# Three expert tiles worked through during the last routing of an attention and mixture-of-experts kernel

## The chip, the cores and the metric

The kernel runs on one core of one Trainium2 chip. The metric is the device time of one launch in microseconds; the times below are of separate launches of the same program.

## The reference

One layer over 4096 nodes of 512 features: masked attention, then a mixture of experts.

```python
x = x + attention(layernorm(x), adj)             # 8 heads of 64; mask: adj or the diagonal
xf = layernorm(x)
logits = xf @ Wg + bg                            # 8 experts
topk_scores, topk_idx = top_k(logits, 2)
topk_w = softmax(topk_scores)
h = gelu(einsum('nd,edh->neh', xf, W1) + b1)     # exact gelu, 512 hidden
y = einsum('neh,ehf->nef', h, W2) + b2
x = x + sum_k topk_w[:, k] * y[:, topk_idx[:, k]]
```

The adjacency is sparse and uneven: a node's edges become fewer with its number, in row and column.

## The kernel before

All of it is in `_fast`, in float32, under a hand-written order: an engine runs its instructions in the order in which the program issues them. (`general` is a fallback for inputs that do not fit, and is not run here.)

Attention. N = 4096 queries are 32 query tiles of P = 128. For each tile the keys that its queries need are gathered into `ring`, a buffer of 24 slots, and worked through two blocks at a time (a *duo*; S duos in all). The loop over n turns keys (`turn`, L733), makes scores (`scores`, L770, Exp on ACT at L777, mask on DVE at L783) and adds values (`values`, L798). After a query tile's last duo, `end_of` puts its closing into later steps with `at(n, i, job)`: `flip_o` (L835), `project` (L843), `residual` (L852, the write to `out` at L854; for the last three tiles on ACT's queue). In a step n >= S, when attention is over, the jobs of a step are ordered by query tile, the latest tile first.

Routing. Query tiles are routed in groups: eight of four would be the plain way, but the last four are split into [28, 29], [30] and [31], so there are groups 0 to 9. `route(g, n)` lays out for a group: `root` (L880 to L899, the layernorm's root on DVE), `norm` (L910, ACT), `flip` (L921, copy L923 to x2T), `gate` (L953, logits added on DVE at L957), `rank` and `place` (L968 to L984, DVE), `number_places` (L990, L991, PE) and `keep_places` (L997), `pick` (L1032 to L1049, with an Exp on ACT at L1044), `finish` (L1058 to L1068) and `scatter` (L1072: the normalised rows, each with its token number, place and weights, go by indirect DMA on POOL to their expert's stretch of `xs_d` in DRAM). `count` holds how many rows each expert has so far. `totals` (L1004 to L1008) counts them all after the last group, and `blanks` writes a blank tile behind each expert's last row (L1020), five on SP's queue and three on ACT's.

`idle(name, n)` (L809) issues n transposes on PE that nothing reads; `idle_0` has 24, `idle_1` 8, `idle_2` 30.

The expert weights, 16 MB, come in eight parts of [128, 8 x 512]: `load_part` (L1158) on SP's queue. Seven parts go into `ring` as its slots come free; the eighth goes into the pool `wff`, which takes the place of the attention's buffers (`s3.close()`) at n == S.

Closing. L1201 loads ACT's gelu table. L1204 to L1239 make the table of the first FULL whole tiles, each with its expert and first row: `tiles_e` is the number of whole 128-row tiles of an expert, `pej` a matmul that spreads the table to all partitions. L1243 to L1255 make the flag that says whether the inputs fitted.

Expert tiles. FULL = 57 whole tiles are certain, whatever the routing: (8192 - 8 x 127) / 128, rounded up. What is left goes in half tiles of 64 rows, two to a *mixed* tile; `halves` (L1299 to L1345) makes their table, `pq_e` being its matmul. The loop `tiles` runs over 57 + 9 = 66 tiles, the mixed ones spread among them. For a tile: `fetch` (L1283, rows from `xs_d` on SP's queue, four tiles ahead, five buffers), `turn` (L1358, copy L1360), `hidden` (L1398, copy L1403), `turn_hidden` (L1409, bias b1 added at L1415, gelu L1420), `second` (L1427, bias b2 added at L1445, weight on ACT at L1449, and L1454: an indirect DMA on POOL that adds the rows to `out`). `warm` (L1353) issues 60 idle transposes ahead of the first tile, between the flag's matmul `pb` and `pq_e`. A mixed tile's second expert has its own copy of weights, loaded by `load_other` (L1375).

The buffers of the closing and routing live in pools that are closed (`s2`) before the pools of the expert loop (`s4`) are opened; both use the same memory.

Of the kernel before, what the change touches and what calls it, by code (L numbers as in the profile page):

```python
# [9 lines left out]
F32 = mybir.dt.float32  # L10
BF16 = mybir.dt.bfloat16
I32 = mybir.dt.int32
U16 = mybir.dt.uint16
F16 = mybir.dt.float16
AF = mybir.ActivationFunctionType
ALU = mybir.AluOpType
# [4 lines left out]
P = 128  # L21
# [54 lines left out]
def _fast(ctx, tc, dram, flag, x, adj, Wks, Wqs, Wvs, Wo, Wg, bg, W1, b1, W2, b2, out):  # L76
# [20 lines left out]
    R = N + P  # L97


    FULL = -(-(2 * N - E * (P - 1)) // P)  # L100
    Q = P // 2
    NB = -(-((2 * N + E * (Q - 1)) // Q) // 2)
    NQ = 2 * (NB - FULL)
    W = D + 4

# [538 lines left out]
    with ExitStack() as s2:  # L644
# [48 lines left out]
        def at(n, i, job):  # L693
            later.setdefault(n, []).append((i, job))
# [119 lines left out]
        group_of = {i: g for g, m in enumerate(groups) for i in m}  # L814
        gst = {}
        closing = {}

        def end_of(i, n):

            hold = {}  # L820

            def scale():
                o = os_[i][:, :, : NP * VW].rearrange("p b (h v) -> p b h v", v=VW)
                r = inverses[:, i].rearrange("p (b h) -> p b h", b=2)
                nc.vector.reciprocal(r, o[:, :, :, KD])
                on = mid.tile([P, 2, NP, KD], F32, tag="on", name=f"on_{i}")
                nc.vector.tensor_mul(
                    on, o[:, :, :, :KD], r.unsqueeze(3).to_broadcast([P, 2, NP, KD])
                )
                hold["on"] = on.rearrange("p b h v -> p (b h v)")  # L830

            def flip_o():
                pt = bank(f"po_{i}", [NP, P])
                for c in range(NP):
                    nc.tensor.transpose(pt[:, c, :], hold["on"][:, ts(c, P)], ident)  # L835
                oT = mid.tile([P, NP, P], F32, tag="oT", name=f"oT_{i}")
                nc.scalar.copy(oT, pt)
                hold["oT"] = oT

            def project():  # L840
                hold["py"] = bank(f"py_{i}", [D])
                for c in range(NP):
                    nc.tensor.matmul(  # L843
                        hold["py"], hold["oT"][:, c, :], wo[:, c, :],
                        start=(c == 0), stop=(c == NP - 1),
                    )

            def residual():
                g = group_of[i]
                m = groups[g]  # L850
                xi = xs_[i][:, :D]
                nc.vector.tensor_add(xi, xi, hold["py"])  # L852
                queue = nc.sync if i < NT - 3 else nc.scalar
                queue.dma_start(out=out[ts(i, P), :], in_=xi)  # L854
                if g not in gst:
                    gst[g] = small.tile([P, 2, 4], F32, tag="mvg", name=f"mvg_{g}")
                k = m.index(i)
                stats = small.tile([P, nc.vector.BN_STATS_DIM], F32, tag="stats", name=f"sb_{i}")
                nc.vector.bn_stats(stats, xi)
                nc.vector.bn_aggr(gst[g][:, :, k], stats)  # L860

            scale()
            at(n + 1, i, flip_o)
            at(n + 2, i, project)
            at(n + 2, i, residual)
            if i == NT - 1:
                at(n + 2, i, lambda: idle("idle_0", 24))
            g = group_of[i]
            if i == groups[g][-1]:
                route(g, n + 3)  # L870

        def route(g, n):
# [181 lines left out]
            def finish():  # L1054
# [9 lines left out]
                for k in range(G):  # L1064
# [2 lines left out]
                    nc.vector.tensor_copy(xi[:, D + 2 : D + 3], inv[:, k : k + 1])  # L1067
                    nc.vector.tensor_copy(xi[:, D + 3 : D + 4], less[:, k : k + 1])  # L1068

            def scatter(k, j):  # L1070
                nc.gpsimd.memset(tick, 0.0)
                s = nc.gpsimd.indirect_dma_start(  # L1072
                    out=xs_d,
                    out_offset=bass.IndirectOffsetOnAxis(
                        ap=hold["slot"][:, j, k : k + 1], axis=0
                    ),
                    in_=xs_[m[k]], in_offset=None,
                )
                for t in scatters:
                    tc.declare_no_dep(s.ins, t.ins, reason="other rows")  # L1080
                scatters.append(s)
# [15 lines left out]
            at(n, m[-1], place)  # L1097
            at(n + 1, m[-1], number_places)
            at(n + 1, m[-1], keep_places)
            if g == len(groups) - 1:  # L1100
                at(n, m[-1], lambda: idle("idle_1", 8))
                at(n + 1, m[-1], totals)
                at(n + 1, m[-1], lambda: idle("idle_2", 30))
            if g == len(groups) - 2:
                n += 1
            at(n + 2, m[-1], pick)
# [54 lines left out]
        def duo(f, n):  # L1161
            if n < S:
                for s in duos[n]:
                    f(s)

        issue(AHEAD, -1)
        duo(turn, 0)
        duo(turn, 1)
# [3 lines left out]
        while n < S or any(k >= n for k in later):  # L1172
            duo(scores, n + 1)
            duo(turn, n + 3)
            if n == S - 1:
                for _, job in later.pop(n, []):
                    job()
            duo(values, n)
            if n < S:
                end = steps[duos[n][-1]]  # L1180
                if end["last"]:
                    end_of(end["i"], n)
                    load_xi(end["i"])
                issue(n + 1 + AHEAD, n)
                load_weights(n)
            todo = later.pop(n, [])
            if n >= S:
                todo.sort(key=lambda job: -job[0])
            for _, job in todo:
                job()  # L1190
            if n == S:
                s3.close()
                wff = ctx.enter_context(tc.tile_pool(name="wff", bufs=1))
                for k in range(PARTS, DC + HC):
                    load_part(k, wff.tile([P, SW], F32, name=f"w_{k}"))
            n += 1


# [4 lines left out]
        whole = tail.tile([P, E], I32, name="whole_e")  # L1203
        nc.vector.tensor_single_scalar(whole, number, 7, op=ALU.logical_shift_right)  # L1204
        tiles_e = tail.tile([P, E], F32, name="tiles_e")
        nc.vector.tensor_copy(tiles_e, whole)
        upto = tail.tile([P, E], F32, name="upto_e")
        nc.vector.tensor_tensor_scan(
            upto, tiles_e, none, initial=0.0, op0=ALU.add, op1=ALU.add
# [7 lines left out]
        nc.vector.scalar_tensor_tensor(  # L1217
            ej[:, 1:2], ej[:, 1:2], -float(P), nth128, op0=ALU.mult, op1=ALU.add
        )
        diag = tail.tile([P, 2, P], BF16, name="diag")  # L1220
        nc.vector.tensor_mul(
            diag, ident.unsqueeze(1).to_broadcast([P, 2, P]),
# [14 lines left out]
        )  # L1237
        nc.vector.tensor_copy(table[:, FULL:], pos[:1, :FULL])
        nc.vector.tensor_add(pos[:, :FULL], pos[:, :FULL], nth.to_broadcast([P, FULL]))  # L1239

        inv = inverses.rearrange("p i h -> p (i h)")
        fl = tail.tile([P, NT * H], F32, name="fl")
# [17 lines left out]
    with ExitStack() as s4:  # L1260
# [35 lines left out]
        def halves():  # L1296
# [3 lines left out]
            nc.vector.tensor_scalar(low, low, -1.0, float(FULL), op0=ALU.mult, op1=ALU.add)  # L1300
            nc.vector.tensor_scalar_max(low, low, 0.0)
            nc.vector.tensor_tensor(low, low, tiles_e, op=ALU.min)
            nc.vector.tensor_scalar_mul(low, low, 2.0)
            nc.vector.tensor_scalar_add(number, number, float(Q - 1))
            nc.vector.tensor_single_scalar(number, number, 6, op=ALU.logical_shift_right)
# [43 lines left out]

        def warm():  # L1350
            pt = ps_t.tile([P, HC, P], F32, tag="t", name="pt_warm")
            for k in range(60):
                nc.tensor.transpose(pt[:, k % HC, :], ident, ident)  # L1353

        def turn(b):
# [133 lines left out]
                    load_other(mixed.pop(0))  # L1489


        LIKELY = (2 * N // Q + E // 2 - 2 * FULL + 1) // 2
        seq = list(range(FULL))
        for k in range(LIKELY):
            seq.insert(7 + 6 * k, FULL + k)
# [559 lines left out]
```

## Time and profile before

| | |
|---|---|
| median of 4 runs | 2269.18 us (2266.57 to 2276.54) |
| the profiled execution | 2277.96 us, span 2276.1 us |
| mean granted TensorE clock in it | 0.937 |
| PE busy in the span | 2066.7 us, 91% |
| DVE, ACT, POOL busy | 972.3, 794.1, 560.6 us |

The profile is of one execution. PE is the matmul engine (PEld its weight loads), DVE the vector engine, ACT the scalar engine, POOL the one that issues indirect DMAs, SP a queue that issues plain ones. A line of a timeline gives start, duration, engine, source line, operation, output <- inputs, shapes and count, and in brackets the idle time before it and what ended that. A line of the windows gives a stretch, its length, each engine's busy time with its instructions (PE, PEld, DVE, ACT, POOL), the granted TensorE clock, the DMA engines' share and GB/s. All times of a view are counted from the span's start.

### The profile page before, as it was taken

How to read it: one execution, taken by the hardware profiler on the slowest of the kernel's cores; microseconds unless marked ns; L12 is line 12 of the kernel's file. 1: busy time of each engine (PE TensorE's matmuls, PEld its weight loads, DVE VectorE, ACT ScalarE, POOL GpSimd, SP SyncE). 2: the span in 40 equal slices, each digit the busy share in tenths (PEclk: the TensorE clock that was granted, in tenths of full speed). 3: DMA queues.
4: the chain of work that ended last, by engine and by line, in shares of the span. 5: the costliest groups of instructions: out<-in, count | busy, mean ns of one | idle time of the engine just before them, and what ended most of it. 6: DMA issues, size and time to landing. Idle time of an engine off the chain costs nothing. (4 is left out here: it accounts for less than half of the span.)

```text
span 2276.1 us, 59936 instructions
## 1 busy us (share of the span) xinstructions
PE 2066.7 (91%) x25581; PEld 1361.6 (60%) x25581; DVE 972.3 (43%) x2519; ACT 794.1 (35%) x1166; POOL 560.6 (25%) x715
## 2 busy tenths in 40 slices
PE   9899999979899988988979889798887999999997
PEld 4344444468777766777757667577665444444443
DVE  3455655425333533444434445245354333333332
ACT  3233333135343533534524435244431222222221
POOL 2000000043333343243243331523311222222221
PEclk9999999989998989988989889799888999999999
DMA  9778773396676766667667584766687455555543
GB/s 373 251 264 257 263 263 121 102 367 218 221 236 201 238 224 224 208 218 252 218 215 240 171 275 167 255 214 193 219 281 253 105 106 114 111 119 136 109 73 44
DMA packets 193602, 462.00 MB, mean 203 GB/s; under 512 B 30384, under 2 KB 46768, under 8 KB 193200
## 3 DMA queue, kind: packets, MB, share of 16 engines
q0 software_dynamic: 66784, 248.65, 36.2%
q1 hardware_dynamic: 102096, 178.04, 24.0%
q10 hardware_dynamic: 24448, 31.38, 4.0%
q8 instruction: 206, 3.38, 0.6%
q14 instruction: 68, 0.56, 0.1%
HBM read 385.37 MB, written 72.64 MB: 201 GB/s over the span
## 5 line engine op out<-in xcount | busy, mean ns | idle before, releaser
L706 POOL DMA_INDIRECT ring<-kv_d,idx x361 | 351.8, 974 | 1102.4 <-PE list L303 433.8
L770 PE MATMUL ps<-q,kT 64*64 64x64 f32 (+1 forms) x10224 | 396.5, 247 | 91.5 <-issue 83.9
L777 ACT ACTIVATE pr<-ps 128x1024 f32<-128x1024 f32 x270 | 272.3, 1024 | 559.2 <-PE ps L770 436.1
L783 DVE SCALAR_TENSOR_TENSOR pr<-t,pr 128x1024 f32<-128x1024 uint16 x238 | 286.3, 1223 | 416.6 <-ACT pr L777 340.1
L770 PEld LDWEIGHTS ps<-q,kT 64*64 64x64 f32 (+1 forms) x10224 | 328.6, 154 | 167.0 <-issue 152.0
L798 PE MATMUL o<-ring,pr 128*64 128x65 f32 x8640 | 315.0, 229 | 32.8 <-issue 32.6
L798 PEld LDWEIGHTS o<-ring,pr 128*64 128x64 f32 x8640 | 286.1, 143 | 68.4 <-issue 66.2
L733 PE MATMUL pkT<-ident,ring 128*128 128x128 f32 x1572 | 234.3, 300 | 31.5 <-issue 18.8
L1398 PE MATMUL ph<-ring,xT 128*128 (+1 forms) x528 | 238.2, 594 | 0.8 <-ACT xT L1360 0.8
L733 PEld LDWEIGHTS pkT<-ident,ring 128*128 128x128 f32 x1572 | 189.5, 153 | 58.1 <-issue 29.9
L735 ACT COPY kT<-pkT 128x512 f32<-128x512 f32 (+1 forms) x270 | 199.7, 787 | 35.5 <-PE pkT L733 12.7
L1454 POOL DMA_INDIRECT out_dram<-y,r x66 | 101.9, 1544 | 371.2 <-ACT y L1449 278.3
L1427 PE MATMUL py_e<-ring,hT 128*128 (+1 forms) x396 | 182.3, 596 | 1.6 <-ACT hT L1420 1.6
L1398 PEld LDWEIGHTS ph<-ring,xT 128*128 128x128 f32 (+1 forms) x528 | 91.3, 183 | 99.8 <-issue 98.7
L1449 ACT ACTIVATE y<-y,wt 128x512 f32<-128x512 f32 x66 | 47.6, 722 | 269.9 <-DVE y L1445 230.1
L614 PE MATMUL pv<-wv,xT 128*128 128x512 f32 x256 | 131.8, 611 | 0.0
L614 PE MATMUL pk<-wk,xT 128*128 128x512 f32 x256 | 125.7, 610 | 0.7 <-ACT xT L408 0.7
L843 PE MATMUL py<-wo,oT 128*128 128x512 f32 x256 | 123.1, 625 | 2.6 <-ACT part L936 1.9
L599 PE MATMUL pq<-xT,wq 128*128 128x512 f32 x256 | 123.1, 603 | 0.0
L1403 DVE COPY h<-ph 128x512 f32<-128x512 f32 x66 | 45.6, 692 | 169.9 <-PE ph L1398 169.9
L1427 PEld LDWEIGHTS py_e<-ring,hT 128*128 128x128 f32 (+1 forms) x396 | 67.2, 183 | 76.0 <-issue 74.1
L1072 POOL DMA_INDIRECT xs_d<-x,slot_i x58 | 66.4, 1145 | 174.4 <-DVE x L1068 57.1
(280 smaller groups left out, 1904.7 us busy)
## 6 DMA issues: line engine op xcount, KB each, us to landing
adj<-in_adj_dram SPq DMA_DIRECT2D x64, 1024.0 KB
wo<-in_L_ffn_W_dram SPq DMA_DIRECT2D x72, 256.0 KB
kv_d<-kvr ACTq DMA_DIRECT2D x32, 516.0 KB
ring<-kv_d SPq DMA_DIRECT2D x32, 516.0 KB
r<-xs_d SPq DMA_DIRECT2D x57, 258.0 KB
ring<-in_L_ffn_W_dram SPq DMA_DIRECT2D x56, 256.0 KB
xt<-in_x_dram SPq DMA_DIRECT2D x32, 256.0 KB
q_d<-qT ACTq DMA_DIRECT2D x32, 256.0 KB
```

The source lines that it names most:

```text
L599: nc.tensor.matmul(pq, w["q"][:, c, ts(p, P)], xTs[b][:, c, :], start=(c == 0), stop=(c == DC - 1),)
L614: nc.tensor.matmul(pk, xTs[b][:, c, ts(t, P)], w[n][:, c, :], start=(c == 0), stop=(c == DC - 1),)
L706: nc.gpsimd.indirect_dma_start(out=g, out_offset=None, in_=kv_d, in_offset=bass.IndirectOffsetOnAxis(ap=idx[i // GL][:, i % GL, a : a + 1] ...
L733: nc.tensor.transpose(pk[:, x * NP + p, :], g[:, ts(p, P)], ident)
L735: nc.scalar.copy(kT[:, : nk * NP], pk[:, : nk * NP])
L770: nc.tensor.matmul(ps[c : c + nk, r, p * P + x * nq : p * P + (x + 1) * nq], kT[r * KD : (r + 1) * KD, p, c : c + nk], q[r * KD : (r + 1) ...
L777: nc.scalar.activation(pr.rearrange("p h q -> p (h q)"), ps.rearrange("p r f -> p (r f)"), AF.Exp)
L783: nc.vector.scalar_tensor_tensor(pr, st["t"].unsqueeze(1).to_broadcast([P, H, P]), 0.0, pr, op0=ALU.is_gt, op1=ALU.mult,)
L798: nc.tensor.matmul(o[c * HALF : (c + 1) * HALF, h // NP, (h % NP) * VW : (h % NP + 1) * VW], pr[:, hd * NP + p, c * HALF : (c + 1) * HALF] ...
L843: nc.tensor.matmul(hold["py"], hold["oT"][:, c, :], wo[:, c, :], start=(c == 0), stop=(c == NP - 1),)
L1398: nc.tensor.matmul(ph[a], xTs[b][:, c, a], w, start=(c == 0), stop=(c == DC - 1), skip_group_check=b >= FULL,)
L1427: nc.tensor.matmul(py[a], hTs[b][:, c, a], w, start=(c == 0), stop=(c == HC - 1), skip_group_check=b >= FULL,)
```

## The change

After group 5 (24 query tiles routed, at least 768 rows in the fullest expert) a small table is made: the expert that is fullest then (`who`), and the first row of its first three whole tiles. These EARLY = 3 tiles are fetched at n == S, their rows and one bias row on ACT's queue, and are worked through between the steps of the last routing and in the closing, by the functions `early_turn`, `early_hidden`, `early_turn_hidden`, `early_gelu` and `early_second`. The loop's tables leave them out (`taken`, `skip`): FULL is 54, NB is 65, and the nine mixed tiles stay. `idle_0` and `idle_2` are gone, and `warm` has 12 transposes instead of 60.

```diff
-    FULL = -(-(2 * N - E * (P - 1)) // P)
+    EARLY = 3
+    FULL = -(-(2 * N - E * (P - 1)) // P) - EARLY
     Q = P // 2
-    NB = -(-((2 * N + E * (Q - 1)) // Q) // 2)
+    NB = -(-((2 * N + E * (Q - 1)) // Q) // 2) - EARLY
...
-            if i == NT - 1:
-                at(n + 2, i, lambda: idle("idle_0", 24))
...
+            def early_table():
+                pn = bank("pn_early", [E])
+                nc.tensor.matmul(pn, ones, count, start=True, stop=True)
+                most = small.tile([P, 1], F32, bufs=1, name="most")
+                nc.vector.tensor_reduce(most, pn, axis=AX.X, op=ALU.max)
+                at_ = small.tile([P, E], F32, bufs=1, name="at_most")
+                nc.vector.tensor_scalar(
+                    at_, pn, most, -float(E * R), op0=ALU.is_equal, op1=ALU.mult
+                )
...
+                for k in range(EARLY):
+                    nc.vector.tensor_scalar(
+                        posA[:, k : k + 1], nth, row0, float(k * P), op0=ALU.add, op1=ALU.add
+                    )
+                    nc.vector.tensor_scalar_add(
+                        tableA[:, 1 + k : 2 + k], row0[:1], float(k * P)
+                    )
+                closing.update(taken=taken, who=who, posA=posA, tableA=tableA)
...
+                if g > EG:
+                    late.append(s)
...
             at(n + 1, m[-1], keep_places)
+            if g == EG:
+                at(n + 1, m[-1], early_table)
             if g == len(groups) - 1:
                 at(n, m[-1], lambda: idle("idle_1", 8))
                 at(n + 1, m[-1], totals)
-                at(n + 1, m[-1], lambda: idle("idle_2", 30))
...
+        def early_fetch(pool):
+            t = closing["tableA"]
+            ea["e"] = nc.values_load(
+                t[:, 0:1], engines=(mybir.EngineType.Activation, mybir.EngineType.PE,
+                                    mybir.EngineType.DVE),
...
+            for k in range(EARLY):
+                first = nc.values_load(
+                    t[:, 1 + k : 2 + k], engines=(mybir.EngineType.Activation,), min_val=0,
...
+                s = nc.scalar.dma_start(out=r, in_=xs_d[bass.ds(first, P), :])
+                for t_ in late:
+                    tc.declare_no_dep(s.ins, t_.ins, reason="other rows")
+                ea["r", k] = r
+            nc.scalar.dma_start(
+                out=ea["b"], in_=b2[bass.ds(ea["e"], 1), :].partition_broadcast(P)
+            )
+        def early_turn(k):
+            pt = bank(f"pt_early{k}", [DC, P])
+            for c in range(DC):
+                nc.tensor.transpose(pt[:, c, :], ea["r", k][:, ts(c, P)], ident)
+            nc.scalar.copy(ea["xT"][k % 2], pt)
+        def early_hidden(k):
+            ph = bank(f"ph_early{k}", [HID])
+            for c in range(DC):
+                nc.tensor.matmul(
+                    ph, ea["xT"][k % 2][:, c, :], wparts[c][:, bass.ds(ea["e"], 1), :],
+                    start=(c == 0), stop=(c == DC - 1),
+                )
+            nc.scalar.copy(ea["h"][k % 2], ph)
+        def early_turn_hidden(k):
...
+            nc.vector.tensor_tensor(
+                ea["hT"][k % 2], pt,
...
+        def early_gelu(k):
+            nc.scalar.activation(ea["hT"][k % 2], ea["hT"][k % 2], AF.Gelu)
+        def early_second(k):
...
+            nc.vector.tensor_add(y, py, ea["b"])
+            nc.scalar.mul(y, y, wt)
+            nc.gpsimd.indirect_dma_start(
+                out=out,
+                out_offset=bass.IndirectOffsetOnAxis(ap=r[:, D : D + 1].bitcast(I32), axis=0),
+                in_=y, in_offset=None, compute_op=ALU.add,
+            )
+
+        at(S + 1, -1, lambda: early_turn(0))
+        at(S + 1, -1, lambda: early_hidden(0))
+        at(S + 2, -1, lambda: early_turn(1))
+        at(S + 2, -1, lambda: early_turn_hidden(0))
+        at(S + 7, -1, lambda: early_hidden(1))
+        at(S + 7, -1, lambda: early_turn(2))
...
             if n == S:
                 s3.close()
                 wff = ctx.enter_context(tc.tile_pool(name="wff", bufs=1))
+                last = [wff.tile([P, SW], F32, name=f"w_{k}") for k in range(PARTS, DC + HC)]
+                early_fetch(s2.enter_context(tc.tile_pool(name="earlies", bufs=1)))
                 for k in range(PARTS, DC + HC):
-                    load_part(k, wff.tile([P, SW], F32, name=f"w_{k}"))
+                    load_part(k, last[k - PARTS])
...
-        nc.vector.tensor_copy(tiles_e, whole)
+        nc.vector.tensor_sub(tiles_e, whole, closing["taken"])
...
+        skip = tail.tile([P, 1], F32, name="skip")
+        nc.vector.tensor_scalar(
+            skip, ej[:, 0:1], closing["who"], float(P * EARLY), op0=ALU.is_equal, op1=ALU.mult
+        )
+        nc.vector.tensor_add(ej[:, 1:2], ej[:, 1:2], skip)
...
         nc.vector.tensor_add(pos[:, :FULL], pos[:, :FULL], nth.to_broadcast([P, FULL]))
+        early_gelu(0)
+        early_turn_hidden(1)
+        early_gelu(1)
+        early_second(0)
+        early_hidden(2)
+        early_turn_hidden(2)
+        early_second(1)
+        early_gelu(2)
+        early_second(2)
...
-            for k in range(60):
+            for k in range(12):
                 nc.tensor.transpose(pt[:, k % HC, :], ident, ident)
```

In the order of the steps, by the rule above (latest query tile first, the early jobs with tile number -1 last): step S + 1 is `project` and `residual` of tile 31, `flip` of 30, `number_places` of group 7, then `early_turn(0)` and `early_hidden(0)`; step S + 2 is `root` of 31, `gate` of 30, `pick` of group 7, then `early_turn(1)` and `early_turn_hidden(0)`; step S + 7 is `number_places` of group 9, `totals`, `finish` of group 8, then `early_hidden(1)` and `early_turn(2)`; the last `pick` comes at S + 8. The y of the three early tiles shares one buffer.

## Prediction

> **What bounds the kernel now.** I read the page first: PE is busy for 91% of the span. In the loop over the expert tiles it never rests, so a tile taken out of that loop is worth its full period.
>
> ```profile
> span 2276.1 us, 59936 instructions
> PE 2066.7 (91%) x25581; PEld 1361.6 (60%) x25581; DVE 972.3 (43%) x2519; ACT 794.1 (35%) x1166; POOL 560.6 (25%) x715
> ```
>
> Then PE's timeline at the start of that loop. The eight `ph` matmuls of two neighbouring tiles start at 1754.76 and 1762.51: 7.75 us a whole tile.
>
> ```profile
> 1754.76 3.60 PE L1398 MATMUL ph<-ring,xT 128*128 x8
> ...
> 1762.51 1.88 PE L1398 MATMUL ph<-ring,xT 128*128 x4
> ```
>
> Then the stretch that the change fills, from the last attention values (1696) to the loop's first `ph` (1741.85), on PE:
>
> ```profile
> 1702.14 5.28 PE L843 MATMUL py<-wo,oT 128*128 128x512 f32 x8 [0.73 <-ACT oT L837]
> 1707.26 2.78 PE L809 MATMUL idle<-ident 128*128 128x128 f32 x24
> 1709.88 0.60 PE L921 MATMUL px<-ident,xn 128*128 128x128 f32 x4
> ...
> 1711.21 1.06 PE L953 MATMUL pl<-wg,x2T 128*128 128x8 f32 x8 [0.70 <-ACT x2T L923]
> 1714.91 0.66 PE L921 MATMUL px<-ident,xn 128*128 128x128 f32 x4 [2.65 <-ACT xn L910]
> ...
> 1725.71 0.27 PE L1226 MATMUL pej<-diag,ones 128*128 128x256 bf16 x1 [0.83 <-DVE ej L1217]
> 1731.20 0.16 PE L1254 MATMUL pb<-badb,ones 128*128 128x1 bf16 x1 [5.22 <-DVE badb L1252]
> 1731.60 8.93 PE L1353 MATMUL pt_warm<-ident 128*128 128x128 f32 x60 [0.24 <-DVE flag L1255]
> ...
> 1741.85 0.70 PE L1398 MATMUL ph<-ring,xT 128*128 x1 [0.80 <-ACT xT L1360]
> ```
>
> PE has 29.92 us busy of 46 here, but 18.1 of them are idle transposes (2.78 + 1.95 + 4.42 + 8.93). So 34 us hold no work: room for 3 x 7.75. What sets the length is a chain over DVE, ACT and PE by turns. ACT's part, where the change puts copies:
>
> ```profile
> 1714.06 0.80 ACT L910 ACTIVATE xn<-x,shift,root 128x512 f32<-128x512 f32 x1
> 1722.76 0.20 ACT L1044 ACTIVATE xn<-diff 128x1 f32<-128x1 f32 x1 [1.50 <-DVE diff L1043]
> 1726.21 1.28 ACT L1201 ACT_TABLE_LOAD   x1 [3.25 <-DVE ej L1217]
> ```
>
> Last, the windows. These four follow the trace's clock steps; the last columns are granted clock, DMA share and GB/s. After waits of some 4 us PE is granted half its clock for about 6.8 us, and DMA is full from 1698 to 1715.
>
> ```profile
> 1698.50:1705.30 6.80, 4.28 (x8) 2.23 (x9) 2.85 (x12) 1.30 (x2) 5.72 (x12) 0.50 1.01 373
> 1705.40:1715.50 10.10, 6.75 (x47) 5.25 (x45) 5.82 (x32) 1.49 (x3) 0.37 (x2) 1.00 1.04 400
> 1729.30:1736.00 6.70, 4.56 (x22) 4.40 (x22) 4.99 (x30) 0.00 (x0) 0.00 (x0) 0.50 0.61 192
> 1736.10:1750.00 13.90, 12.70 (x70) 8.50 (x69) 2.79 (x11) 1.80 (x3) 0.00 (x0) 1.00 0.97 343
> ```
>
> **The change, part by part.** The sum is made against the profiled execution, 2277.96 us (span 2276.1 and 1.9 around it); the median of the four runs shown is 2269.18, 0.39% lower, and I put the difference on that.
>
> Removed from the loop: FULL goes from 57 to 54, the mixed tiles stay nine, so 3 x 7.75 = 23.2 us go. The loop's start moves the other way, and the rest counts by how much.
>
> The early table: 15 small DVE instructions of about 0.2 us at the routing of group 5, right after L997 at 1565.4. DVE then waits 2.91 us for ACT; 3 us fit that but for a trifle, and one more PSUM bank is turned. Between 0 and 2; I take 0.5.
>
> The rows. ACT is done with L910 for tile 30 at 1702.8; with two register loads (0.5 and 0.4 us, as L1015 on ACT) the first row DMA goes at about 1703.4. How long it takes is bounded by two rows: the first `r` of the loop (issued 1733.86 on an empty queue, its bytes moved between 1734.85 and 1736.7: 2.9 us), and the residual's write on this very queue (issued 1708.23; none of its 0.26 MB moved before 1711.8, all by 1714: 5.4 us). The second lies in the same crowd: rows at 1708.8. The Trainium skill (DMA: Bandwidth & Descriptors, Anatomy of one DMA) gives 2.0 us plus bytes over 436 GB/s, an estimate of 2.6 us for 258 KB; by it the rows would be there at 1706.0 and this wait would be nothing.
>
> An issue can also be held. The eight loads of the last weight part stand on SP from 1703.50 to 1714.2, 1.34 us apart where an issue alone is 0.33: each waits for an earlier landing. ACT's four new issues and the residual's DMA behind them draw on the same landings. Never held, ACT passes the residual's issue at 1708.6; taking turns one to one with SP, near 1716. I take 1711.2, nearer to the first, since PE's and POOL's other traffic thins out. Queued behind it on ACT are tile 30's x2T copy and the new xT copy.
>
> So: x2T(30) and xT0 (0.6 each) to 1712.5, first hidden 3.6 to 1716.2, then gate(30), queued behind it on PE, 1.06 to 1717.3; before it ended at 1712.27: +5.0. (With idle_0 gone, DVE's place and root come 1.4 us sooner; that is lost here, because the gate is last.) Exp of group 7 and the xT1 copy stand ahead of norm(31) on ACT, which comes at 1719.1 instead of 1714.06. DVE has one hT add (0.7) more. The last logits (L957, before 1718.22) come at 1723.4: +5.2.
>
> Second hidden and third turn stand ahead of the last Exp on ACT: from the logits 2.3 to `pn`, 3.6 of matmul, 0.7 at half clock partly, copies 0.7 and 0.6 with hand-overs: 8.0 from the logits where it was 4.54. +3.4; the Exp at 1722.76 + 8.6 = 1731.4. The DVE chain behind it waits for it, plus two added instructions: `pej` at 1725.71 + 9.0 = 1734.7.
>
> From the Exp on, ACT needs 4.95 us for blanks' issues, table load and gelu as before (1722.76 to 1727.71), then the first early gelu 0.63: 1736.9. From there PE and its partners go by turns, each instruction at its own row: second(0) 3.6, and 1.8 for half clock after a wait of 4 us (half of the 6.8 us stretch falls on work), to 1742.4; hidden(2) 3.6 to 1746.0; copy, transposes, hand-overs 1.5 to 1747.5; second(1) 3.6 to 1751.1; its add (0.69), scaling (0.72), then gelu(2) (0.63) behind that on ACT, 2.4 to 1753.5; second(2) 3.6 plus 1.8 at half clock to 1758.9.
>
> Then the hole. The loop's pools take the place of pools that hold the early rows and y; I read that as: the loop's first row fetch waits until the last early add into `out` has landed. Add and scaling 1.9; POOL's add to its landing 4.9 (first L1454 starts at 1756.30, its 0.26 MB have moved by 1760.8 and the next fetch follows at 1761.4); fetch 0.4 + 2.9; turn and copy 1.5: 1770.5. PE has little between (pb, 12 transposes, `pq_e`), so the first hidden starts at half clock: 2.0 more, 1772.5 in effect. Before: 1741.85. Shift 30.6 + 0.5 - 23.2 = +7.9. The 48 dropped warm transposes, 48 x 0.11 = 5.3 us, no longer bind, since rows are later than they.
>
> The Trainium skill (TensorE: Matmul & The Clock Gate, What's actually happening) says that the gate falls to half after an idle window of about 3.4 us and rises after one busy window; by it alone each half-clock stretch would cost at most 1.7 us. The windows above show 6.8 us, of which part fell on idle work.
>
> **Rivals.** *Even* (within 0.3%, 6.8 us): ACT is not held (xT0 at 1710.2, -2.3) and the clock stays full in the closing (-1.8, -1.8, -2.0): 0.0. For it: DMA is full only to 1715. Against: the waits of 2.4 and 9 us stand in the code's order.
>
> *Faster:* the early work fills PE's waits as meant, since the loop's row fetch need not wait for the early adds. One place, the hole: with ACT not held and full clock second(2) ends at 1758.9 - 2.3 - 3.6 = 1753.0; its add (0.9), then DVE's flags and halves (1.65 + 0.5 + 3.75, L1243 to L1326) bind, `pq_e`, turn and copy 1.9: first `ph` at 1761.7, net -3.4; with gate(30) at its old time (the 2.7 left of 5.0) -6.1, with the last Exp not held either (3.4) -9.5. It decides from a first `ph` before 1741.85 + 23.2 - 6.8 = 1758.3. For it: 34 us of room. Against: three tiles' chain of copy, gelu and add has a hand-over after every 3.6 us of matmul.
>
> *Slower yet:* ACT held to 1716, +4.8 on the main line: +12.7; with 2 in the attention, +15.
>
> *Not what it says:* the three tiles are whole in any case (some expert has at least 6144/8 = 768 rows by then), so the loop does lose three.
>
> **How the numbers follow.** Main line and slower yet 0.55, even 0.29, faster 0.16; 0.3% is about what a measurement of this kernel can tell from no change, and these are its three sides. Predicted: 2269.2 + 7.9 = 2277.1. Low end 2269.2 - 6.2 = 2263.0, into the faster case; high end +14.8 = 2284.0. The main line alone: 2272 to 2284.
>
> **What would show it.** Right: the loop shows 63 `ph` groups at 7.75 us, the first at 1765 to 1775; gate(30) behind the first early hidden; the last Exp behind an early copy; half clock in the closing; SP's first `r` after the third early add. Wrong: first `ph` before 1758, early rows at PE's hand before the residual's matmuls end, the first `r` ahead of the early adds, or PE at full clock throughout.

## The result: 0.34% slower, and the profile after

The changed kernel takes 2278.22 us (median of 52 runs, 2262.35 to 2291.6) beside 2272.03 of the kernel before (78 runs): ratio 1.0034, 95% interval 1.0022 to 1.0045. By that ratio it is 7.7 us slower, by the two medians 6.2. The forecast was 2277.1 us, 7.9 us slower. The profiled execution of the change took 2289.28 us with a span of 2287.5, one of its slower ones; what follows compares stretches inside the traces, not the two totals.

Two stretches carry the case, and both are named again for every experiment. The *closing* runs from the transposes of tile 31's attention (`po`, 1700.29 before, 1703.29 after; "+10" below means 10 us after it) to the first hidden matmul of the loop (`ph`). The *loop* runs from there to the end. The closing grew from 41.56 to 70.81 us, the loop shrank from 534.23 to 513.38: +29.25 and -20.85, together +8.4. (Ahead of the closing the profiled execution of after was 3.0 us later as well.)

The page's first lines, of after:

```profile
span 2287.5 us, 59737 instructions
...
PE 2058.2 (90%) x25480; PEld 1348.0 (59%) x25480; DVE 972.8 (43%) x2534; ACT 795.0 (35%) x1169; POOL 559.0 (24%) x715
```

PE's timeline through the closing, of after (start, duration, the wait ahead of it and what ended it):

```profile
1713.67 5.40 PE L1243 MATMUL ph_early<-ring,xT_early 128*128 x8 [1.34 <-ACT xT_early L1238]
1718.90 0.95 PE L955 MATMUL pl<-wg,x2T 128*128 128x8 f32 x8
...
1738.33 0.37 PE L1363 MATMUL pej<-diag,ones 128*128 128x256 bf16 x1 [3.46 <-DVE diag L1358]
...
1740.98 4.85 PE L1265 MATMUL py_early<-ring,hT_early 128*128 x6 [1.42 <-ACT hT_early L1260]
...
1757.06 2.84 PE L1265 MATMUL py_early<-ring,hT_early 128*128 x6 [2.12 <-ACT hT_early L1260]
1759.74 1.02 PE L1265 MATMUL py_early<-w,hT_early 128*128 x2
1764.04 0.18 PE L1400 MATMUL pb<-badb,ones 128*128 128x1 bf16 x1 [3.28 <-DVE badb L1398]
...
1772.21 1.09 PE L1505 MATMUL pt_e<-ident,r 128*128 128x128 f32 x4 [3.64 <-DMA r<-xs_d]
1774.10 6.21 PE L1545 MATMUL ph<-ring,xT 128*128 x8 [0.80 <-ACT xT L1507]
...
1781.77 3.69 PE L1545 MATMUL ph<-ring,xT 128*128 x8
```

All four places of the forecast are there. Gate(30) (`pl`) stands right behind the first early hidden, which took 5.40 us, where a later one takes 3.60: the granted clock was 0.50 from 1714.40 to 1717.81. `pej` comes at +35.0, where before had it at +25.4. Between the last early second (ends 1760.8) and the first `ph` lie 13.3 us in which PE is busy for 3.3. And that first `ph` takes 6.21 us where the next takes 3.69.

ACT's timeline shows the last routing's Exp (L1046) directly behind two early copies:

```profile
1734.47 0.58 ACT L1247 COPY h_early<-ph_early 128x512 f32<-128x512 f32 x1 [3.58 <-PE ph_early L1243]
1734.96 0.58 ACT L1238 COPY xT_early<-pt_early 128x512 f32<-128x512 f32 x1
1735.44 0.21 ACT L1046 ACTIVATE xn<-diff 128x1 f32<-128x1 f32 x1
```

And SP's waits in the stretch name what the hole waited for: the first row fetch (L1429) stood until the early adds into `out` had landed (us in total, times, longest).

```profile
SPq L1429 <- DMA out_dram<-y_early,r_early: 27.3, 1, 27.3
```

### The profile page after: what moved, and what is told of

It reads as the page before. It is cut to its first block, busy times and chain, and to the rows that moved or that the text cites. A ratio compares the mean times of both kernels' runs of the same rounds, so it can differ in the third digit from the quotient of the medians.

```text
span 2287.5 us, 59737 instructions
## 1 busy us (share of the span) xinstructions
PE 2058.2 (90%) x25480; PEld 1348.0 (59%) x25480; DVE 972.8 (43%) x2534; ACT 795.0 (35%) x1169; POOL 559.0 (24%) x715
## 5 line engine op out<-in xcount | busy, mean ns | idle before, releaser
L1545 PE MATMUL ph<-ring,xT 128*128 (+1 forms) x504 | 229.9, 599 | 0.8 <-ACT xT L1507 0.8
L1601 POOL DMA_INDIRECT out_dram<-y,r x63 | 97.1, 1541 | 350.1 <-ACT y L1596 257.1
L1574 PE MATMUL py_e<-ring,hT 128*128 (+1 forms) x378 | 174.1, 596 | 1.6 <-ACT hT L1567 1.6
L1107 POOL DMA_INDIRECT xs_d<-x,slot_i x58 | 65.5, 1130 | 181.0 <-DVE x L1070 57.1
```

The source lines that it names most:

```text
L1545: nc.tensor.matmul(ph[a], xTs[b][:, c, a], w, start=(c == 0), stop=(c == DC - 1), skip_group_check=b >= FULL,)
L1574: nc.tensor.matmul(py[a], hTs[b][:, c, a], w, start=(c == 0), stop=(c == HC - 1), skip_group_check=b >= FULL,)
```

## The experiments

The runs came from several chips; on some of them the attention ahead of this stretch is granted a higher clock and every kernel takes some 230 us less, so a kernel is compared by its ratio to the kernel before on the same chip, and by closing and loop of its own trace. Each closing and loop is that of one execution, and no trace of the kernel before was kept on the faster chips.

| kernel | early tiles | closing | loop | sum | median, us | ratio to before, 95% |
|---|---|---|---|---|---|---|
| before | 0 | 41.56 | 534.23 | 575.8 | 2272.0 | 1 |
| the change | 3 | 70.81 | 513.38 | 584.2 | 2278.2 | 1.0034 [1.0022, 1.0045] |
| `hole` | 3 | 66.90 | 514.48 | 581.4 | 2278.4 | 1.0025 [1.0001, 1.0048] |
| `pool_queue` | 3 | 67.60 | 516.13 | 583.7 | 2276.9 | 1.0016 [0.9997, 1.0035] |
| `exp_free` | 3 | 69.72 | 513.57 | 583.3 | 2280.4 | 1.0047 [1.0017, 1.0077] |
| `clock` | 3 | 74.32 | 509.61 | 583.9 | 2280.0 | 1.0031 [1.0005, 1.0057] |
| `gate_first` | 3 | 67.37 | 514.44 | 581.8 | 2050.1 | 1.0022 [0.9998, 1.0046] |
| `one_tile` | 1 | 45.78 | 528.38 | 574.2 | 2045.3 | 1.0006 [0.9982, 1.0031] |
| `two_tiles` | 2 | 59.12 | 521.16 | 580.3 | 2051.2 | 1.0030 [1.0007, 1.0053] |
| `before_warm30` | 0 | 39.92 | 536.46 | 576.4 | 2047.5 | 1.0017 [0.9992, 1.0041] |
| `best1` | 1 | 45.37 | 526.39 | 571.8 | 2044.6 | 1.0002 [0.9985, 1.0020] |
| `best2` | 2 | 50.52 | 520.96 | 571.5 | 2035.5 | 0.9961 [0.9942, 0.9981] |
| `best3` | 3 | 60.80 | 513.69 | 574.5 | 2044.0 | 1.0006 [0.9992, 1.0019] |
| `late2` | 2 | 40.91 | 520.81 | 561.7 | 2027.6 | 0.9926 [0.9900, 0.9952] |

Most intervals are some 0.2% (5 us) either way, wider than the 1 to 4 us that single waits are worth; the steps are therefore read from the traces, and the ratios only say whether the sum went the same way.

### The hole: y and the last early rows in memory that the loop does not take over

```diff
-ea["y"] = pool.tile([P, D], F32, name="y_early")
+ea["y"] = ea["keep"].tile([P, D], F32, name="y_early")
 ...
-r = pool.tile([P, W], F32, name=f"r_early{k}")
+r = (ea["keep"] if k == EARLY - 1 else pool).tile([P, W], F32, name=f"r_early{k}")
 ...
+ea["keep"] = ctx.enter_context(tc.tile_pool(name="kept", bufs=1))
```

> The changed kernel with y_early and r_early2, the two buffers that the last early add still reads, in memory that the expert loop's pools do not take over. Measure: the closing, from the transposes of po for tile 31 to the loop's first ph (41.6 us in the kernel before, 70.8 in the changed one), and the loop from there to the end (534.2 and 513.4). Theory: SP's first r waits for the landing of the last early add only because of the memory; then it goes some 5 us sooner (after the scaling of y at about +59 instead of +65.5 from po), pq_e (at +65.1) binds instead, first ph at +66.8, 4 us sooner, total 4 us less. Rival: SP's first r waits for the scatters' and blanks' rows anyway, closing 70.8 and no change.

The closing fell by 3.9 us to 66.90. SP issued the first row at 1752.34, now ahead of the last early add and no longer 5.3 us behind it; SP's wait went from 27.3 to 20.8:

```profile
SPq L1430 <- DMA out_dram<-y_early,r_early: 20.8, 1, 20.8
```

So the fetch did wait for the landing of the last add, because of where its memory lay. The wait that is left is for an earlier add: it ends at 1751.1, after the second add (issued 1746.59) and before the third (1753.17), and the second one's rows still lie in the old pool. DVE's flags and halves are now nearly as late as the row, as PE's timeline of that run shows: `pq_e` waits for DVE, and the row comes half a microsecond later.

```profile
1758.02 0.20 PE L1480 MATMUL pq_e<-diag,ones 128*128 128x22 bf16 x2 [2.38 <-DVE diag L1474]
1758.73 0.72 PE L1506 MATMUL pt_e<-ident,r 128*128 128x128 f32 x4 [0.51 <-DMA r<-xs_d]
```

DVE's chain is the next bound which the faster rival had named. With it so near, freeing the row alone was worth 3.9 us in this trace, though the row was issued 6.5 us sooner (+59.0 for +65.5).

### ACT's queue: early rows and bias fetched on POOL's

```diff
-s = nc.scalar.dma_start(out=r, in_=xs_d[bass.ds(first, P), :])
+s = nc.gpsimd.dma_start(out=r, in_=xs_d[bass.ds(first, P), :])
```

The register loads and the bias go to POOL with them.

> The changed kernel with the early rows and bias fetched on POOL's queue instead of ACT's. Theory: ACT is no longer held, x2T of tile 30 follows the residual at once (1.5 us sooner, at +7.7 from po instead of +9.25), and the routing's logits come 1 to 2 us sooner; total -1 to -2. Rival: the rows' landing sets early_turn(0), not ACT's queue; then POOL's issues, a microsecond each, bring the rows no sooner and the first early hidden starts as now, at +10.4.

The residual's issue on ACT came at +7.4 instead of +8.8, tile 30's copy at +7.9 instead of +9.25, gate(30) at +13.6 instead of +15.6, `pej` at +31.9 instead of +35.0; the closing fell by 3.2 us. ACT's timeline names what tile 30's copy waited for, in after and then in `pool_queue`:

```profile
1712.54 0.58 ACT L925 COPY x2T<-px 128x512 f32<-128x512 f32 x1 [7.21 <-DMA r_early<-xs_d]
...
1696.26 0.58 ACT L925 COPY x2T<-px 128x512 f32<-128x512 f32 x1 [5.83 <-DVE x L856]
```

The hold on ACT was real, and 1.4 us long at its end. The other 1.7 us at `pej` are not the hold's: 0.6 of them came because the first early hidden needed 4.8 us there, a stop of 0.83 for weights included, and 5.4 in the change; for the rest no cause was found.

### The last Exp: the second early hidden behind `pej`

```diff
-at(S + 7, -1, lambda: early_hidden(1))
-at(S + 7, -1, lambda: early_turn(2))
 ...
 early_gelu(0)
+early_hidden(1)
+early_turn(2)
 early_turn_hidden(1)
```

> The changed kernel with early_hidden(1) and early_turn(2) taken from step S + 7 and put behind the table's matmul pej. Theory: their copies no longer stand ahead of the last Exp on ACT, so Exp and pej come 3 to 3.5 us sooner (pej at +31.6 from po instead of +35.0), but the 4 us of matmul then stand in the closing, where PE waits only for ACT's gelu table: first ph within 1.5 us of +70.8, either way. Rival: the hold of the Exp costs its full 3.4 us, and the first ph comes at +67.4.

The Exp stood behind no copy and came 4.40 us after the last logits instead of 7.45, so the hold was 3.05 us long (3.4 in the forecast). `pej` came at +31.6 (+35.0), and the closing was 69.72 us, 1.1 less than the change's; 0.8 of both was there at the last logits, ahead of what the edit moved. What was taken from ahead of `pej` stood behind it: the moved hidden needed 5.59 us there, in part at half clock, for 3.60 at full. A place for PE work is worth only what PE would have waited there anyway.

### The clock at the loop's start: idle transposes in the hole

```diff
 early_second(2)
+idle("idle_s", 30)
 ...
-warm()
+warm(36)
 halves()
+warm(36)
```

> The changed kernel with idle transposes in the closing's waits: 30 after the last early second, 36 instead of 12 after the flag's matmul, 36 more after pq_e. Measure: granted clock from the last early second to the second ph, and the duration of the first ph (6.21 us in the changed kernel, 3.70 in the kernel before). Theory: the clock is at full when the loop starts, the first ph takes 3.7, and the first ph starts no later than now unless the added transposes overrun the row's landing by up to 1 us; total 2 to 3 us less. Rival: the half clock there costs nothing that is seen in the total, because the loop's first tiles wait for bias and weights; the first ph may be faster, the stretch to the third ph is not.

The first `ph` took 3.70 us instead of 6.21, and the loop was 509.61 us, 3.8 shorter. The closing of that one trace was 74.32. Of its excess of 3.5 over the change's 70.81, 3.3 arose ahead of every added transpose: PE waited 5.75 us for DVE at the last routing (1703.78), which put `pn` 1.5 us later than in the change, and the second early hidden behind it took 6.10 us instead of 4.31. From `pej` to the end the trace is 3.5 us shorter than the change's (545.6 and 549.1). But the ratio, 1.0031, does not tell the kernel from the change. So the half clock in the loop's start is real, and with the idle work the first `ph` ran at full clock; that the total gains by it is not shown.

### Gate(30) ahead of the first early hidden

```diff
-at(S + 1, -1, lambda: early_hidden(0))
-at(S + 2, -1, lambda: early_turn(1))
-at(S + 2, -1, lambda: early_turn_hidden(0))
+at(S + 2, -1, lambda: early_hidden(0))
+at(S + 4, -1, lambda: early_turn(1))
+at(S + 4, -1, lambda: early_turn_hidden(0))
```

> The first early hidden is queued behind tile 30's gate instead of ahead of it, the second early turn and the first turn of hidden values two steps later. Theory (gate(30) stood 5 us late for its place behind this hidden, and all of the last routing follows from it): gate(30)'s matmuls 4 us sooner after the transposes of tile 31 (15.6 us in the change), pej 3 to 4 us sooner (35.0 in the change), closing 66 to 68 us, so 3 to 4 us under the change. Rival (the early matmuls are PE's time wherever they stand, what is gained at the gate is lost behind it): pej at 34 to 35, closing 70 to 71, the change's time.

Gate(30) at +10.9 (+15.6), `pej` at +30.8 (+35.0), closing 67.37: the closing is the theory's, and `pej` came 4.2 us sooner where it had 3 to 4. So 3.4 us of the closing came from the place of these groups in PE's order; up to 0.6 of it is clock, since the second early hidden took 3.70 us there and 4.31 in the change. The ratio does not tell the kernel from the change.

### One tile, two tiles

```diff
-EARLY = 3
+EARLY = 1        # in the other kernel 2; the steps of the missing tiles are gone
```

> One early tile instead of three (EARLY = 1; the second and third turns, hiddens and seconds are gone, and the loop has 56 whole tiles). Theory (the first early tile carries the fixed price: rows held on ACT's queue, gate(30) behind the first early hidden, and the hole in which the loop's first row fetch waits for the last early add; every further tile costs in the closing about what it saves in the loop): from the transposes of tile 31's attention to the first hidden matmul of the loop 49 to 52 us (41.6 before, 70.8 with three), the loop from there about 528 (534.2 before, 513.4 with three), so 1 to 3 us over before, and 5 to 7 us under the change. Rival (a single tile fits into PE's waits for nothing, and only the second and third are too many): closing at most 44 us, 4 to 6 us under before. Other rival (the whole of the price is the fixed one): closing 62 us or more, slower than the change by 10.

> Two early tiles instead of three (EARLY = 2). Theory (a further tile costs in the closing about what it saves in the loop): closing 62 to 65 us, loop 521, sum within 2 us of the change's. Rival (the third tile is the one that does not fit): closing under 60 us, 4 us or more under the change. Rival (the fixed price is all): closing 69 to 71, 7 us over the change.

My theory fell here. I had expected a large price for the first tile and the loop's own price for each further one. By the table (its traces are of different chips) the first tile cost 4.2 us of closing and saved 5.9 of loop, the second cost 13.3 and saved 7.2, the third cost 11.7 and saved 7.8. The first pays its way in the traces, the later two do not. (By its numbers `two_tiles` met its first rival, closing under 60 us; but that rival blamed the third tile, and the second cost more. The ratios, 1.0006 and 1.0030, show no gain for either kernel.) Of the second tile's price 1.7 us is clock, the first early hidden taking 5.40 us in `two_tiles` and 3.70 in `one_tile`. DVE's timeline of `two_tiles` names another 3.5 us: second(1) ended on PE at 1516.5, and y(1) could not be written until y(0), in the one buffer they share, had been added into `out`.

```profile
1519.97 0.69 DVE L1282 TENSOR_TENSOR y_early<-py_early,b_early 128x512 f32<-128x512 f32 x1 [5.50 <-DMA out_dram<-y_early,r_early]
```

DVE's flags and halves, and with them `pb` and `pq_e`, stood behind that, and so did the last early add, for whose landing the fetch waits.

### The 48 dropped warm transposes, in the kernel before

```diff
-for k in range(60):
+for k in range(30):
     nc.tensor.transpose(pt[:, k % HC, :], ident, ident)
```

> The kernel before with 30 instead of 60 warm transposes ahead of the loop. The forecast put nothing on the change's 48 dropped ones, because its rows come later than they do. In before, they may bind: the row has landed at 1736.7, the halves' diag is ready at 1735.3, and the warm transposes end at 1740.3. Theory (they bind, at 0.11 us each at full clock): the first hidden matmul 2.5 to 3.3 us sooner, closing 38 to 39 us instead of 41.6, 3 us under before. Rival (they only fill a wait, or the clock drops without them): closing within 0.7 us of before, or the loop longer by as much; no change.

The closing was 39.92 instead of 41.56, the loop 536.46 instead of 534.23: no gain in sum. PE's timeline shows the rows as the next bound at once, and the first `ph` in part at half clock:

```profile
1500.22 0.20 PE L1332 MATMUL pq_e<-diag,ones 128*128 128x22 bf16 x2
1503.06 1.08 PE L1358 MATMUL pt_e<-ident,r 128*128 128x128 f32 x4 [2.64 <-DMA r<-xs_d]
1504.94 5.97 PE L1398 MATMUL ph<-ring,xT 128*128 x8 [0.80 <-ACT xT L1360]
```

That fits the forecast's zero for the dropped transposes: they covered a wait, and without them the first `ph` took 5.97 us for 3.70.

### All the waits together, with one, two and three tiles

```diff
+rowp = ctx.enter_context(tc.tile_pool(name="rowp", bufs=5))   # rows, early and loop's
-r = work.tile([P, W], F32, tag="row", bufs=5, name=f"r_{b}")
+r = rowp.tile([P, W], F32, tag="row", name=f"r_{b}")
+ea["y"] = [ea["keep"].tile([P, D], F32, name=f"y_early{k}") for k in range(min(2, EARLY))]
 ...                                     # early rows and bias on POOL's queue
+for t in ea.get("reads", []):           # group 6's scatters and later
+    tc.declare_no_dep(s.ins, t.ins, reason="other rows")
+at(S + 2, -1, lambda: early_hidden(0))
+at(S + 4, -1, lambda: early_turn_hidden(0))
 ...                                     # DVE's flags and halves here, then:
 early_second(0)
```

> One early tile, with everything that the runs so far showed as a wait taken away: the rows of the early tile and of the loop come from one pool that stands over the whole end (no wait of the loop's first fetch for the early add), y in a pool of its own, early rows and bias on POOL's queue, the last routing's scatters not behind the early read, the first early hidden behind tile 30's gate, DVE's flags and halves ahead of the early y instead of behind it, 30 idle transposes in the wait before pej, 24 warm ones. Theory (what the early tile cost was these waits; the loop's first fetch then waits for the last blank row alone, at some 34 us after the transposes of tile 31, as in the run with one tile): closing 37 to 39 us (41.6 before, 45.8 with one tile so far), loop 526.5 to 528.5 (534.2 before), so 9 to 12 us under before, ratio 0.994 to 0.996. Rival (the hand-overs from engine to engine are the cost, not these waits): closing 44 to 46, no change against before.

> The same with two early tiles: the second hidden stands in PE's wait ahead of pej, its copy on ACT behind the last Exp and the blank rows, its second behind the first one's, two buffers for y. Theory (both seconds and the second hidden lie in the stretch in which the loop's first row is on its way in any case): closing 39 to 43 us, loop 518.5 to 520.5, so 13 to 17 us under before, ratio 0.9925 to 0.9943. Rival (PE is the bound from the last routing on, every further tile costs what it saves): closing 46 or more, no better than with one.

> The same with three early tiles, as the change has: the third hidden and second follow the first second on PE. Theory (the third finds no wait left: 3.6 us of hidden, 3.6 of second and 0.6 of transposes for the 7.75 that it saves): closing 47 to 51 us, loop 511 to 513, so within 3 us of two tiles, and 13 to 17 us under the change's own 584 of closing and loop. Rival (the order and the memory were not what cost the change its gain): closing 63 or more.

The closings were 45.4, 50.5 and 60.8: 6 to 10 us above the upper ends that I expected, though `best2` beat the kernel before (0.9961). `best1` and `best2` came to lie where their rivals had them (hand-overs, or PE, as the bound). PE no longer stood for the row or for DVE's halves, and yet `pej` came at +32.8 to +33.8. PE's timeline of `best2` shows why, and two lines of ACT's:

```profile
1478.41 1.06 PE L955 MATMUL pl<-wg,x2T 128*128 128x8 f32 x8 [1.38 <-ACT x2T L925]
1479.33 2.50 PE L1247 MATMUL ph_early<-ring,xT_early 128*128 x4
1485.64 3.75 PE L1247 MATMUL ph_early<-ring,xT_early 128*128 x4 [3.82 <-DMA ring<-in_L_ffn_W_dram]
1490.79 1.11 PE L923 MATMUL px<-ident,xn 128*128 128x128 f32 x4 [1.39 <-ACT xn L912]
...
1489.43 0.59 ACT L1254 COPY h_early<-ph_early 128x512 f32<-128x512 f32 x1 [8.59 <-PE ph_early L1247]
1489.92 0.81 ACT L912 ACTIVATE xn<-x,shift,root 128x512 f32<-128x512 f32 x1
```

The first hidden stopped half way for the other half of W1, which landed 16.9 us after tile 31's transposes (in `one_tile` the same hidden started at +9.5 and did not stop). Behind it on PE stood tile 31's transposes (`px`), and behind its copy on ACT norm(31): all of the last routing waited for a weight that only the early tile wanted. That the weights came later because the scatters no longer waited for the early rows and moved beside them is likely: six scatters start at +1.8 in `best2` and at +9.1 in `pool_queue`, where the rows lie on the same queue and the same half of W1 was there by +11.8. It was not tried by itself.

The third tile cost 10.3 us of closing over the second and saved 7.3: in this order it costs more than it saves, and the ratios agree (0.9961 and 1.0006).

### The first early hidden behind the last routing's matmuls

The edit is shown against `best2`. Besides these lines the copies of the hiddens move with them, the second tile's y lies in memory of the first one's xT, and `warm` has 2 transposes instead of 12.

```diff
-at(S + 2, -1, lambda: early_hidden(0))
-at(S + 4, -1, lambda: early_turn_hidden(0))
-at(S + 7, -1, lambda: early_hidden(1))
 ...
+at(S + 1, -1, lambda: idle("idle_0", 12))
+at(S + 2, -1, lambda: idle("idle_2", 10))
+at(S + 7, -1, lambda: early_hidden(0))
 ...
+early_turn_hidden(0)
 early_gelu(0)
+early_hidden(1)
```

> Two early tiles as in the last run, but the first early hidden stands behind the last matmul of the last routing (pn), where PE waits for DVE's chain to pej, and not behind tile 30's gate; the second one follows pej; 12 and 10 idle transposes fill the place it left. In the last runs the first hidden stopped half way for 4 us on PE, for parts of W1 that landed only 17 us after the transposes of tile 31, and norm(31) on ACT and its transposes stood behind it. Theory (that stop, in order ahead of the last routing, is what kept pej at 32.8 to 33.8 us after the transposes of tile 31, where before has 25.4): pej at 22 to 26, closing 37 to 42 us (50.5 in the last run with two tiles), loop 518.5 to 521, so 13 to 18 us under before, ratio 0.991 to 0.994. Rival (the weights land late for every place, and the two hiddens and seconds behind pn take what the routing gains): closing 47 to 51, no better than the last run with two tiles.

All of the theory's numbers held: `pej` at +25.1, closing 40.91, loop 520.81, ratio 0.9926 [0.9900, 0.9952]. This kernel is 15 us faster than before by the ratio, 13 by the medians (2040.9 before on that chip), and by its ratio it beats the change as well. PE's timeline of it, from the last routing on:

```profile
1480.31 5.43 PE L1249 MATMUL ph_early<-ring,xT_early 128*128 x8 [0.37 <-DMA w<-in_L_ffn_W_dram]
1485.58 0.27 PE L1374 MATMUL pej<-diag,ones 128*128 128x256 bf16 x1
...
1486.91 3.60 PE L1249 MATMUL ph_early<-ring,xT_early 128*128 x8
...
1495.20 2.82 PE L1274 MATMUL py_early<-ring,hT_early 128*128 x6
...
1499.99 0.64 PE L1512 MATMUL pt_e<-ident,r 128*128 128x128 f32 x4
1501.42 3.70 PE L1552 MATMUL ph<-ring,xT 128*128 x8 [0.80 <-ACT xT L1514]
```

The first hidden fills, in part at half clock (5.43 us), the very wait that before spent on 30 idle transposes ahead of `pej`; the second hidden and both seconds run while blank rows, scatters and the loop's first rows are on their way (SP issues the first row at 1494.48). Two whole tiles have left the loop, and the closing is as long as before. In this trace tile 31's projection ran at full clock (3.70 us, 5.40 in `best2`), but gate(30) came no sooner for it (+10.3, +9.7 in `best2`); tile 31's last transposes behind it came at +13.3 instead of +22.0. So the 8.75 us at `pej` arose between the two, where the first hidden and its stop had been.

## Why the forecast was right, step by step

Times are counted from tile 31's transposes of each trace (the forecast's from 1700.29).

| step of the sum | forecast | measured |
|---|---|---|
| first early row issued | +3.1 | +2.0 |
| its landing | 5.4 after | at most 6.3 after (PE takes it at 1711.67) |
| ACT free of the issues | +10.9 | +9.2 |
| first early hidden | +12.2, 3.6 long | +10.4, 5.4 long |
| gate(30) ends | +17.0 | +16.6 |
| last logits | +23.1 | +24.7 |
| last Exp | +31.1 | +32.2 |
| `pej` | +34.4 | +35.0 |
| second(2) ends | +58.6 | +57.5 |
| first row fetch issued | +65.4 | +65.5 |
| first `ph` | +70.2 | +70.8 |
| half clock in it | 2.0 | 2.5 (7.67 to the next `ph`, 5.16 in `clock`) |
| loop | -23.2 + 2.0 | -20.85 |

The main line held from end to end, but several of its terms were off and cancelled, which is luck. ACT was held for 1.7 us less than I took. And half clock cost 7.1 us on real work where I had put 5.6 in three places, or 6.3 if the 0.7 "at half clock partly" ahead of the last Exp is counted: 1.8 on the first hidden (5.40 for 3.60), where I had none, 0.7 on the second, 2.1 on second(0) (from 1740.98 to 1746.68, where second(1) takes 3.60), none on second(2), where I had 1.8, and 2.5 on the loop's first. Two of the half-clock windows of after, in which the last figures are granted clock, DMA share and GB/s:

```profile
1738.22:1745.05 6.83, 5.30 (x10) 2.67 (x10) 2.25 (x10) 2.52 (x4) 0.89 (x1) 0.50 0.58 214
...
1765.53:1779.18 13.65, 7.14 (x17) 3.50 (x15) 3.75 (x25) 0.58 (x1) 0.00 (x0) 0.50 0.79 232
```

The size of that term was near, its places were a guess. Half clock "after waits of some 4 us" was too narrow a reading: before has one more such window, and in its closing PE had waited no longer than 2.65 us ahead of it. The first hidden of after came behind waits of 1.47 and 1.34.

```profile
1715.60:1722.40 6.80, 5.91 (x30) 5.68 (x31) 4.84 (x39) 0.79 (x2) 4.17 (x8) 0.50 0.50 189
```

Three more steps of the sum were off. From gate(30)'s end to the last logits the trace has 8.1 us where I had 6.1. I had charged DVE 0.7 for its first early hT add, but DVE stood 2.46 us idle ahead of that add (1724.05), and PE waited 3.04 us for group 8's `chosen` queued behind it; what the add waited for is not settled, since the `px` that the profile names was over by 1723.0. From `pej` to the end of second(2) it has 22.4 where I had 24.2. From there to the fetch it has 8.0 where I had 6.8: the third y stood some 0.9 us for the shared buffer, a wait that I had put at nothing. The early table is not visible beyond 0.5 us: the routing's places of group 5 came 4.3 us later in after, just before the table ran, and those of group 6 came 4.7 later. (*Slower yet* with 2 us for that table adds up to +14.2, not +15.)

Of the rivals, *even* and *faster* named the right places. *Faster* needed several holds gone at once to reach 9.5 us under before. One at a time they gave 3.9 us of closing (the hole), 3.2 (ACT), 3.4 (the gate) and 1.1 (the Exp), and none of them alone made up for the 8.4. What I did not see was the step that gave the most among the runs, 9.6 us of closing from `best2` to `late2`: that the first early hidden need not stand ahead of the last routing at all, and that one wait there holds two engines' queues. The clause against *faster*, "three tiles' chain of copy, gelu and add has a hand-over after every 3.6 us of matmul", is not what decided: `late2`, with two tiles, has those hand-overs too, and gains.

The Trainium skill (DMA: Bandwidth & Descriptors, Anatomy of one DMA) had 2.6 us as an estimate for a row of 258 KB, by a fit to transfers that POOL issues, where this row went over ACT's queue; the first early row took up to 6.3 here, nearer to the residual's write in the same crowd (5.4), which the sum went by. The skill (TensorE: Matmul & The Clock Gate, What's actually happening) lets the clock rise after one busy window of some 3.4 us, and the trace of after agrees: it has half clock for 3.41 us where the first hidden filled the window (1714.40 to 1717.81), and for 13.65 us where PE was busy for only 7.14 and filled no more than the end. My estimate from that page, at most 1.7 us for a stretch, was low: 1.8 on the first hidden, 2.1 on second(0) and 2.5 at the loop's start.

## What to carry to other kernels

Work put into another stage's waits must stand behind that stage's own chain in every in-order queue, copies and DMA issues included; what it waits for itself (here weights that land late) must be waited for last. Ask of every buffer it uses whose memory comes next and who waits for its last reader: one shared y and one pool boundary cost 3.5 and 3.9 us here. Then move as many units as find a wait and no more: two tiles gained 13 to 15 us in the last order; in the order before it a third cost 10.3 us for 7.3.

## What was not expected of the hardware

The same kernel before takes 2272 us on one chip (that of the first four experiments) and 2041 to 2044 on three others, with a mean granted clock of 0.94 against 0.98; in the attention PE's matmuls were busy for 773 us of 896 on the one and 666 of 711 on the other (the run with 30 warm transposes), at a granted clock of 0.90 and 0.99. Why one chip is granted less there was not found out.

A transfer issued into this crowd lands late: the blank rows in `late2`, the last of them issued by 1487.00, kept SP's first row waiting until 1494.2, 7.2 us later (DMA share 1.05 in the 7 us ahead, 0.79 in these), and W1's last parts in `best2`, issued by +3.5, were waited for until +16.9 (DMA share 1.03 and more from +3.2 on).
